# A two-layer attention kernel on one core: GpSimd issues its own store, maxima of a second unit go beside the last feed-forward, and one load of the output path comes sooner

## The chip, the cores and the metric

The kernel runs on one core of one Trainium2 chip. The metric is the device time of one execution in microseconds (us). Five engines matter: PE (TensorE, matmul), DVE (VectorE), ACT (ScalarE), POOL (GpSimd) and SP (SyncE, which here only issues DMA transfers). Each engine works through its own list of instructions strictly in order and waits on semaphores for the others.

## The reference

Two identical layers on x (4 batches of 512 tokens, width 320) with a context (4 x 1601 tokens, width 192). Each layer is self attention, cross attention and a gated feed-forward, each behind a layer norm and added to x; 20 heads of 16.

```python
h1 = _ln(x, n1_g, n1_b)
x = _attn(h1, h1, q1, k1, v1, o1_w, o1_b, heads) + x
h2 = _ln(x, n2_g, n2_b)
x = _attn(h2, context, q2, k2, v2, o2_w, o2_b, heads) + x
h3 = _ln(x, n3_g, n3_b)
proj = h3 @ ff_w1 + ff_b1
a, g = jnp.split(proj, 2, axis=-1)
ff = a * jax.nn.gelu(g, approximate=False) @ ff_w2 + ff_b2
return ff + x          # _attn: softmax(q k^T * 16**-0.5) v, then @ wo + bo
```

## The kernel before

**Units.** The attention is cut into units: one unit is four heads of one batch (five units a batch, so 20 self units and 20 cross units a layer, then four feed-forward units, `ff`). A self unit has 4 chunks of 128 keys, a cross unit 13. For each chunk PE makes the scores of four heads (tile `st`, line 1324), ACT takes their exponential (`pr`, L1334), and one chunk later PE multiplies by the values (`av`, L1350).

**Maxima.** The softmax subtracts each query's exact maximum, so before a unit can be scored, its scores are made once more only to be reduced: PE writes `sps` (L1076), DVE reduces it to `nmax` (self) or `pm` (cross) (L1087). A self unit has 16 such tiles, four to a round. `max_end` then turns the maxima into rows, and SP sends them to `nrows` (L1171, four small transfers a unit), which the next unit's scores need. `giver` decides whose maxima go beside the unit at work: `coming` are the units ahead, `ahead` those it may take; beside attention the rounds of maxima share the four row groups of PE with the scores, beside a feed-forward they stand alone.

**Sums.** A unit's `av` results are summed over its chunks in a tile `o`: the first chunk is copied by ACT (L1364), each later one is copied by ACT to `vo` (L1369) and added by POOL (L1370). There are two `o` tiles in turn, so the first copy of a unit must wait until the `o` of the unit before the last has been sent away. In the last unit before a feed-forward DVE does both.

**The output path** (`add_finish`). Everything in it goes through one chain named `divide`, first in, first out, with waits counted in rounds of the schedule (`since(i, n)`: n rounds after the i-th mark): `turn` sends `o` (128 x 512) to DRAM (`oway`, L1191, 256 KB); after the fifth unit of a batch `sums` loads the denominators (`den`, L1199), DVE inverts them, `read` loads the numerators and inverses back in three parts (`aT`, `rT`; L1224, L1225), POOL multiplies each part (L1232), and PE projects (`ops`, L1250) into x. The third part is loaded later than the first two, since its buffer is shared with the first. A `turn` that comes due while the third part is waiting stands behind it in the chain.

**Order.** The program is written out by hand by a planner at build time; it fixes the order on every engine. `nc.sync` transfers go out on SP in that order. POOL also makes the high and low halves of the projected q and k (L827, L828), the layer norm of later batches (`hturned`, L625) and bias additions (L618).

Of the kernel before, what the change touches and what calls it, by code (L numbers as in the profile page):

```python
# [25 lines left out]
G, HG = 5, 4  # L26
# [52 lines left out]
def kernel(ctx: ExitStack, tc: tile.TileContext, x, context, ws, out):  # L79
# [18 lines left out]
    nc = tc.nc  # L98
    dma = nc.sync.dma_start
# [313 lines left out]
    def bank(name):  # L413
        i = min(range(NB), key=lambda i: bank_free[i])
        assert bank_free[i] < HELD, name
        t = psum.tile([P, 512], F32, tag=f"bank{i}", name=name)
        bank_of[id(t)] = [i, t, bank_free[i], 0.0]
        bank_free[i] = HELD
        return t

    def written(us, *tiles):
        expect["pe"] = max([expect["pe"]] + [bank_of[id(t)][2] + 0.05 for t in tiles]) + us
        for t in tiles:
            bank_of[id(t)][3] = expect["pe"] + 0.17

    def busy(engine, us, *tiles):
        expect[engine] = max([expect[engine]] + [bank_of[id(t)][3] + 0.05 for t in tiles]) + us
        for t in tiles:
            bank_free[bank_of[id(t)][0]] = expect[engine] + 0.09
# [12 lines left out]
    def add(chain, cost, f, due, ready=yes, soon=yes):  # L442
        chains[chain].append((cost if isinstance(cost, tuple) else (cost,), due, ready, soon, f))
# [356 lines left out]
    def tiles_of(n):  # L800
        return [(f, min(SLOT, n - f)) for f in range(0, n, SLOT)]
# [377 lines left out]
    def add_finish(u):  # L1179

        when = [clock["round"]]

        def since(i, n):
            return lambda: len(when) > i and clock["round"] >= when[i] + n

        def turn():

            way = o_way[u.b % 2]  # L1190
            dma(out=way[:, u.g * HG : (u.g + 1) * HG].rearrange("s j n -> j s n"), in_=u.o)  # L1191
            if u.g == G - 1:
                held["written"] += 1
                errands.append((clock["round"] + 3, yes, sums))

        def sums():

            den = two.tile([P, N], F32, tag="rT", name="den")[:, : H * N // P]
            dma(out=den, in_=o_way[u.b % 2][DH].rearrange("h n -> (h n)").rearrange("(p c) -> p c", p=P))  # L1199
            when.append(clock["round"])  # L1200

            def invert():
                nc.vector.reciprocal(den, den)
                busy("dve", 0.75)
                when.append(clock["round"])

            def save():
                dma(out=r_way[u.b % 2].rearrange("h n -> (h n)").rearrange("(p c) -> p c", p=P), in_=den)
                errands.append((clock["round"] + 3, lambda: held["open"] < 1, read))

            add("divide", LIGHT, invert, r - 20, yes, since(1, 3))
            add("divide", 0.0, save, r - 20, yes, since(2, 1))

        def read():

            held["read"] += 1
            held["open"] += 1
            aT = one.tile([P, 3, N], F32, tag="aT", name="aT")
            way, part = o_way[u.b % 2], {}

            def load(k, at, n):
                heads = slice(at // DH, (at + n) // DH)
                part[k] = two.tile([P, N], F32, tag="rT", name="rT")
                dma(out=aT[:n, k, :], in_=way[:DH, heads])  # L1224
                dma(  # L1225
                    out=part[k][:n],
                    in_=r_way[u.b % 2][heads].rearrange("(o j) n -> o j n", o=1).to_broadcast([DH, n // DH, N]),
                )
                when.append(clock["round"])

            def divide(k, n):
                nc.gpsimd.tensor_tensor(aT[:n, k, :], aT[:n, k, :], part[k][:n], ALU.mult)  # L1232

            for k, at, n in DK[:2]:
                load(k, at, n)
            first, second, third = DK
            add("divide", 0.0, lambda: divide(0, first[2]), r - 20, yes, since(4, 3))
            add("divide", 0.0, lambda: divide(1, second[2]), r - 20)
            add("divide", 0.0, lambda: load(*third), r - 20, yes, since(4, 7))
            add("divide", 0.0, lambda: divide(2, third[2]), r - 20, yes, since(5, 3))  # L1240
            add("divide", 0.0, lambda: end(aT), r - 20)

        def project(aT, t, part):
            cols = slice(part * D // 2, (part + 1) * D // 2)
            ps = bank("ops")
            written(0.93, ps)
            busy("dve", 0.3, ps)
            for k, at, n in DK:
                for f, m in tiles_of(P):
                    nc.tensor.matmul(  # L1250
                        ps[f : f + m, : D // 2],
                        lhsT=aT[:n, k, f * NQ + t * SLOT : f * NQ + t * SLOT + m],
                        rhs=wo[:n, k, cols],
                        start=(k == 0),
                        stop=(k == 2),
                    )
            nc.vector.tensor_tensor(xs[u.b][:, t, cols], ps[:, : D // 2], xs[u.b][:, t, cols], ALU.add)

        def end(aT):
            now = clock["round"]  # L1260
            for t in range(NQ):
                for part in range(2):
                    add(
                        "project", (0.317,) * 3, lambda t=t, part=part: project(aT, t, part),
                        now + 2 + u.nch * t + u.nch // 2 * part, yes, lambda: clock["round"] >= now + 1,
                    )
            add("project", 0.0, done, now + 2 + u.nch * NQ)

        def done():
            held["open"] -= 1  # L1270
            after(u)

        r = when[0]
        add("divide", 0.0, turn, r - 20, lambda: u.g or held["written"] < held["read"] + 2, since(0, 2))


# [346 lines left out]
    def giver(u):  # L1623

        ahead, coming = [], []
        for v in units[u.i + 1 : u.i + AHEAD + 1]:
            if v.kind == "ff":
                break  # L1630
            coming.append(v)
            if v.i <= u.i + 2 and (v.i == u.i + 1 or u.kind != "ff") or v.early:
                ahead.append(v)
                if v.pairs is None:
                    v.pairs = max_pairs(v)
        owed = 0.0
        last = clock["round"]

        def give(h, alone=False):
            nonlocal owed, last  # L1640
            rounds = []
            went = clock["round"] - last if alone else 1
            last = clock["round"]
            total = 0
            most = 0.0
            urgent = None
            for v in coming:
                if v not in ahead:
                    total += v.steps
                    continue  # L1650
                total += left(v)


                rest = v.start - (7 if alone else 4) - clock["round"]
                if rest > 0:
                    most = max(most, (total - rest * (not alone)) / (2 * rest))
                if left(v) and (rest == 1 or alone and rest < 1):
                    urgent = urgent or v
                    owed = max(owed, 1.0 if alone and rest > -4 else (left(v) + 1) // 2)
            owed += most * went if total else 0.0  # L1660
            while owed >= 1.0 and any(left(v) for v in ahead) and not (alone and rounds and rest > -4):
                hand = [v for v in ahead if left(v) and all(v.pairs) and at_hand(v)]
                if not hand and ahead[0].start - 4 - clock["round"] > 1:
                    break
                v = hand[0] if hand else next(v for v in ahead if left(v))
                if u.kind == "self" and ahead[-1].early and urgent is None:

                    v = ahead[-1]
                    if v not in hand:
                        break  # L1670
                at_once(v)
                rounds.append([f for q in v.pairs if q for f in q.popleft()[1]])
                owed -= 1.0
            owed = min(owed, 2.0)
            for v in ahead:
                mine = v.pairs[h % 2]
                if mine and not alone and at_hand(v):
                    return mine.popleft(), rounds
            return (False, []), rounds

        return give
# [46 lines left out]
    for i, u in enumerate(units):  # L1728
# [10 lines left out]
        for k in (3, SOON, AHEAD):  # L1739
            v = units[i + k] if i + k < len(units) else None  # L1740
# [32 lines left out]
```

## Time and profile before

| | |
|---|---|
| three runs | 2933.25 us median (2932.35 to 2940.54) |
| profiled execution | 2933.88 us, of which its span is 2931.7 us |
| mean granted TensorE clock | 0.994 |
| busy in the span | PE 2863.0 us (98%), DVE 2069.9 (71%), ACT 1881.4 (64%), POOL 1299.4 (44%) |
| stages in the span | layer 0: self from 47 us, cross from 381, feed-forward from about 1214; layer 1: self from 1505, cross from 1837, feed-forward from about 2663 to the end |

The share of PE is the time in which some matmul was between its start and its modelled end, so a PE that waits in the middle of a matmul's issue still counts as busy; waits have to be looked for stage by stage. A wait is written as idle time with what ended it, for instance `[3.60 <-POOL aT L1232]`. SP's rows are the issues of transfers; a row of SP that takes several us for `x4` contains waits between its parts. A matmul on full fp32 stands in the trace as two instructions, so an `ops` row `x12` of the program's order is `x24` there.

### The profile page before, as it was taken

The numbers are of one execution on the slowest core, as the hardware profiler recorded it, in microseconds if no ns is written. First come the engines' busy times: TensorE is split into PE (matmuls) and PEld (weight loads), VectorE is DVE, ScalarE is ACT, GpSimd is POOL, SyncE is SP. The second block draws the span as 40 slices with busy tenths as digits, with TensorE's granted clock in tenths as the row PEclk, the third lists the DMA queues.
The fourth block names the chain that finished last, engine by engine and source line by source line (L and its number), as shares of the span: only waits on it lengthen the run. The fifth ranks groups of instructions, "written<-read, shape, count | busy, mean of one in ns | idle before, by whom it ended". The sixth has DMA issues, their size and how long they took to land.

```text
span 2931.7 us, 83446 instructions
## 1 busy us (share of the span) xinstructions
PE 2863.0 (98%) x35018; PEld 1540.3 (53%) x35018; DVE 2069.9 (71%) x4052; ACT 1881.4 (64%) x3733; POOL 1299.4 (44%) x1409
## 2 busy tenths in 40 slices
PE   8999999999999999999999999999999999999999
PEld 4445555555555555355554555555555555544554
DVE  6776888888888888323258678888888888872221
ACT  3767677887887888501138666778878778783000
POOL 3656345555545545211125663456455565551100
PEclk8999999999999999999999999999999999999999
DMA  3443223232232222200113342222221122222000
GB/s 106 113 120 99 68 73 101 59 85 62 49 93 61 54 54 62 84 17 11 42 38 88 99 104 69 58 62 53 62 65 47 50 72 51 53 56 76 22 20 14
DMA packets 163495, 188.59 MB, mean 64 GB/s; under 512 B 61988, under 2 KB 109104, under 8 KB 163120
## 3 DMA queue, kind: packets, MB, share of 16 engines
q1 hardware_dynamic: 162616, 181.69, 24.4%
q8 instruction: 275, 4.51, 0.6%
q10 hardware_dynamic: 472, 1.58, 0.2%
q14 instruction: 100, 0.82, 0.1%
q0 software_dynamic: 32, 0.00, 0.0%
HBM read 55.76 MB, written 29.36 MB: 29 GB/s over the span
## 4 chain that ended last, share of the span: by engine, by line
PE 87%; DVE 5%; POOL 2%; DMA 2%; ACT 2%; issue 1%; SPq 1%; ACTq 0%; POOLq 0%; DVEq 0%
PE av L1350 22%; PE st L1324 20%; PE fps L1435 10%; PE sps L1076 8%; PE yps L1542 6%; PE vps L1035 5%; PE kps L972 4%; PE ops L1250 4%; PE qkps L908 3%; PE fps L1495 3%; DVE nmax L1087 2%; PE qps L947 2%; DMA oway<-o 1%; PE sps L1101 1%; ACT pr L1334 1%
## 5 line engine op out<-in xcount | busy, mean ns | idle before, releaser
L1334 ACT ACTIVATE pr<-st 128x512 f32<-128x512 f32 (+1 forms) x2720 | 1404.5, 604 | 394.3 <-PE st L1324 359.3
L1087 DVE TENSOR_REDUCE pm<-sps 128x1 f32<-128x512 f32 (+1 forms) x1920 | 1147.8, 660 | 138.7 <-PE sps L1076 132.4
L1370 POOL TENSOR_TENSOR o<-o,vo 128x512 f32<-128x512 f32 x576 | 739.8, 1284 | 950.8 <-ACT vo L1369 942.0
L1076 PE MATMUL sps<-kT,q 32*128 32x512 f32 (+1 forms) x4800 | 869.0, 421 | 12.2 <-DMA q<-halves 4.4
L1324 PE MATMUL st<-q,kT 32*128 32x512 f32 (+1 forms) x5120 | 790.7, 420 | 2.8 <-ACT o L1364 2.4
L1350 PE MATMUL av<-pr,vals 128*32 128x512 f32 (+1 forms) x5440 | 734.5, 606 | 35.0 <-ACT pr L1334 13.4
L1324 PEld LDWEIGHTS st<-q,kT 32*128 32x128 f32 (+1 forms) x5120 | 448.5, 180 | 297.4 <-ACT pr L1334 117.5
L1324 PE MATMUL st<-nrows,ones 32*128 32x512 f32 (+1 forms) x2720 | 560.6, 399 | 4.8 <-DMA nrows<-turned 4.7
L1076 PEld LDWEIGHTS sps<-kT,q 32*128 32x128 f32 x4800 | 429.8, 184 | 73.7 <-DVE nmax L1087 14.6
L1087 DVE TENSOR_REDUCE nmax<-sps 128x1 f32<-128x512 f32 x640 | 396.7, 682 | 92.7 <-PE sps L1076 89.2
L1369 ACT COPY vo<-av 128x512 f32<-128x512 f32 x576 | 353.0, 613 | 17.4 <-PE av L1350 10.3
L1506 ACT ACTIVATE gl<-fps,b 128x512 f32<-128x512 f32 x80 | 54.7, 687 | 408.9 <-PE fps L1495 299.1
L1435 PE MATMUL fps<-hT,w 128*128 128x512 f32 x640 | 283.1, 597 | 0.0
L1350 PEld LDWEIGHTS av<-pr,vals 128*32 128x32 f32 (+1 forms) x5440 | 110.9, 108 | 309.9 <-DVE pm L1087 175.8
L1324 PEld LDWEIGHTS st<-nrows,ones 32*128 32x128 f32 (+1 forms) x2720 | 264.6, 180 | 14.8 <-DMA nrows<-turned 6.0
L1507 DVE SCALAR_TENSOR_TENSOR hid<-fps,b,gl 128x512 f32<-128x512 f32 x80 | 59.7, 748 | 242.6 <-ACT gl L1506 240.5
L1435 PEld LDWEIGHTS fps<-hT,w 128*128 128x128 f32 x640 | 119.2, 190 | 155.1 <-issue 152.2
L1542 PE MATMUL yps<-w,hid 128*128 128x320 f32 x640 | 175.5, 434 | 0.0
L1542 PEld LDWEIGHTS yps<-w,hid 128*128 128x128 f32 x640 | 120.6, 190 | 56.1 <-ACT gl L1506 5.3
L1250 PEld LDWEIGHTS ops<-wo,aT 112*32 112x32 f32 (+1 forms) x3072 | 99.3, 111 | 63.1 <-issue 29.5
L1250 PE MATMUL ops<-wo,aT 112*32 112x160 f32 (+1 forms) x3072 | 126.1, 302 | 5.5 <-POOL aT L1232 5.0
L527 POOL TENSOR_SCALAR root<-root 128x4 f32<-128x4 f32 x22 | 5.2, 234 | 266.8 <-DVE root L521 266.7
(91 smaller groups left out, 2544.1 us busy)
## 6 DMA issues: line engine op xcount, KB each, us to landing
kT<-stages SPq DMA_DIRECT2D x80, 400.5 KB
oway<-o SPq DMA_DIRECT2D x80, 256.0 KB
q<-halves SPq DMA_DIRECT2D x80, 256.0 KB
q<-halves SPq DMA_DIRECT2D x27, 512.0 KB
kT<-halves SPq DMA_DIRECT2D x40, 256.0 KB
aT<-oway SPq DMA_DIRECT2D x32, 224.0 KB
rT<-rway SPq DMA_DIRECT2D x32, 224.0 KB
hT<-hturned SPq DMA_DIRECT2D x96, 64.0 KB
```

Of the source, the lines that this page charges most:

```text
L972: nc.tensor.matmul(ps[(i * GT + f) * SLOT : (i * GT + f + 1) * SLOT, :w], lhsT=wk2[:, k, u.g * GD + f * SLOT : u.g * GD + (f + 1) * SLOT], ...
L1035: nc.tensor.matmul(ps[f : f + m, :w], lhsT=u.kvT[:n, k, at + f : at + f + m], rhs=wv[:n, k, h0 * DH : h1 * DH], start=(k == 0), stop=(k == ...
L1076: nc.tensor.matmul(own[0][:, :w], lhsT=u.queries(slice(j * SLOT, (j + 1) * SLOT), e, t), rhs=u.kT[j * SLOT : (j + 1) * SLOT, u.k0 + at : u ...
L1087: nc.vector.tensor_reduce(to, own[0][:, :w], AX.X, ALU.max)
L1250: nc.tensor.matmul(ps[f : f + m, : D // 2], lhsT=aT[:n, k, f * NQ + t * SLOT : f * NQ + t * SLOT + m], rhs=wo[:n, k, cols], start=(k == 0) ...
L1324: nc.tensor.matmul(own[0][:r, :], lhsT=ones[rows, :r] if e == 2 else u.keys(rows, c), rhs=u.rows[rows, :] if e == 2 else u.queries(rows, e ...
L1334: nc.scalar.activation(p[:r], own[0][:r], AF.Exp)
L1350: nc.tensor.matmul(ps[j * SLOT : (j + 1) * SLOT, :], lhsT=columns_of[:r, head : head + SLOT], rhs=pr.pop((c, j))[:r, :], start=True, stop= ...
L1369: nc.scalar.copy(vo, ps)
L1370: nc.gpsimd.tensor_tensor(u.o, u.o, vo, ALU.add)
L1435: nc.tensor.matmul(ps, lhsT=w1[:, k, i * FF + c * P : i * FF + (c + 1) * P], rhs=natural(u.hT[:, k]), start=start, stop=stop,)
L1542: nc.tensor.matmul(ps[:, :D], lhsT=hid[c][:, t * P : (t + 1) * P], rhs=w2[:, c, :], start=(c == 0), stop=(c == NHC - 1),)
```

## The change

Three edits. In `turn`, POOL issues the transfer of `o` itself instead of SP (80 transfers, all of them). In the output path the third load comes 5 instead of 7 rounds after its mark in layer 1; in layer 0 it stays at 7. In `giver`, a feed-forward unit may take the maxima of the next two units instead of the next one; only the last feed-forward of layer 0 has attention units ahead.

```diff
         def turn():

             way = o_way[u.b % 2]
-            dma(out=way[:, u.g * HG : (u.g + 1) * HG].rearrange("s j n -> j s n"), in_=u.o)
+            nc.gpsimd.dma_start(out=way[:, u.g * HG : (u.g + 1) * HG].rearrange("s j n -> j s n"), in_=u.o)
...
-            add("divide", 0.0, lambda: load(*third), r - 20, yes, since(4, 7))
+            add("divide", 0.0, lambda: load(*third), r - 20, yes, since(4, 5 if u.l else 7))
...
-            if v.i <= u.i + 2 and (v.i == u.i + 1 or u.kind != "ff") or v.early:
+            if v.i <= u.i + 2 or v.early:
                 ahead.append(v)
```

**Place A: PE, end of layer 0's last feed-forward and first unit of layer 1.** `yps` is the second feed-forward product, `q_102`, `q_103` and `q_104` are the queries of the first, second and third self unit of layer 1; `-` is the kernel before, `+` the changed one.

```order
 L1542 MATMUL yps<-w_22016,hid 128x320 x4
+L1076 MATMUL sps<-kT_101,q_103 128x512 x8
 L1542 MATMUL yps<-w_22016,hid_22439 128x320 x3
 L1542 MATMUL yps<-w_22016,hid_22440 128x320 x3
 L1542 MATMUL yps<-w_22016,hid 128x320 x4
+L1076 MATMUL sps<-kT_101,q_103 128x512 x8
 L1324 MATMUL st<-q_102,kT_101 128x512 x2
```

```order
 L1350 MATMUL av<-pr,vals 32x512 x4
-L1076 MATMUL sps<-kT_101,q_103 128x512 x8
-L1076 MATMUL sps<-kT_101,q_104 128x512 x16
+L1076 MATMUL sps<-kT_101,q_104 128x512 x8
 L1324 MATMUL st<-q_102,kT_101 128x512 x2
```

Two rounds of four maxima of the second unit now stand before and behind the last `yps` of the feed-forward. One lone round in the first chunk of unit 0 (eight matmuls of a row `x10`) is gone, and the three lone rounds behind its second chunk have become one; the last four maxima of the third unit are done in the first chunk of unit 1. Unit 0 has 5 rounds of maxima instead of 8, not counting the two that moved.

**Place B: the transfer of unit 12's sums in layer 0.** Before, on SP: `o_4279` is the sum of unit 12, `o_4550` of unit 13, the `halves` are the split k and q of later units, the `aT`/`rT` rows are the third load of batch 1.

```order
L1224 DMA aT_4375<-oway1_131 96x1x512
L1225 DMA rT_4625<-rway1_133 96x1x512
L876 DMA kT0_101<-halves_4298 128x1x512
L876 DMA q1_103<-halves_4298 128x1x1024
L1191 DMA oway0_130<-o_4279 4x32x512
L876 DMA q3_136<-halves_4565 128x1x512 x2
L1191 DMA oway0_130<-o_4550 4x32x512
```

The same transfers in the changed kernel, on POOL:

```order
L1370 TENSOR_TENSOR o_4550<-o_4550,vo_4622 128x512
L1370 TENSOR_TENSOR o_4550<-o_4550,vo_4673 128x512
L1370 TENSOR_TENSOR o_4550<-o_4550,vo_4723 128x512
L1232 TENSOR_TENSOR aT_4375<-aT_4375,rT_4625 96x512
L1191 DMA oway0_130<-o_4279 4x32x512
L1191 DMA oway0_130<-o_4550 4x32x512
L827 CAST halves_4791<-halves_4791 128x512
```

Unit 12's transfer has moved behind all of unit 13's additions and the third multiplication on POOL. At the same place of layer 1 the third multiplication and unit 12's transfer stand between the second and the third of those additions.

**Place C: POOL, units 8 and 9 of layer 1**, before and then changed. `o_26178` and `o_26165` are the sum of unit 8, `hturned` is the layer norm of batch 3, `oway1_131<-o_25872` the transfer of unit 7.

```order
L1370 TENSOR_TENSOR o_26178<-o_26178,vo_26254 128x512
L625 TENSOR_SCALAR hturned_26115<-x3_110,mv_25804,root2_25977 128x4x32
L625 TENSOR_SCALAR hturned_26115<-x3_110,mv_25804,root2_25977 128x3x32 x2
L827 CAST halves_26199<-halves_26199 128x512
L828 TENSOR_TENSOR halves_26199<-halves_26199 128x512
L1370 TENSOR_TENSOR o_26178<-o_26178,vo_26321 128x512
L1232 TENSOR_TENSOR aT_25912<-aT_25912,rT_26180 96x512
```

```order
L1370 TENSOR_TENSOR o_26165<-o_26165,vo_26238 128x512
L1232 TENSOR_TENSOR aT_25896<-aT_25896,rT_26099 96x512
L1191 DMA oway1_131<-o_25872 4x32x512
L625 TENSOR_SCALAR hturned_26102<-x3_110,mv_25788,root2_25961 128x4x32
L625 TENSOR_SCALAR hturned_26102<-x3_110,mv_25788,root2_25961 128x3x32 x2
L827 CAST halves_26183<-halves_26183 128x512
L828 TENSOR_TENSOR halves_26183<-halves_26183 128x512
L1370 TENSOR_TENSOR o_26165<-o_26165,vo_26307 128x512
```

The third multiplication comes one piece of layer norm, one split into halves and one addition sooner, and the transfer follows it. On PE the first `ops` of that batch comes one chunk sooner too.

## Prediction

> **What bounds the kernel now.** I read the totals of the page first, then the waits, then the groups by line.
>
> ```profile
> span 2931.7 us, 83446 instructions
> PE 2863.0 (98%) x35018; PEld 1540.3 (53%) x35018; DVE 2069.9 (71%) x4052; ACT 1881.4 (64%) x3733; POOL 1299.4 (44%) x1409
> ACT o L1364 <- DMA oway<-o: 7.6, 2, 3.9
> PE ops L1250 <- POOL aT L1232: 5.0, 2, 3.6
> ACT vo L1369 <- POOL o L1370: 5.8, 6, 2.7
> SPq L1191 <- POOL o L1370: 311.0, 65, 10.5
> SPq L1171 <- DMA oway<-o: 6.0, 4, 2.3
> ```
>
> A row of waits gives the sum, the count and the longest. PE is the bound: its visible idle time is 2931.7 − 2863.0 = 68.7 us, and no PE work is removed. So a gain can only come from waits of PE that these edits end, and each is a few us. SP stands 311.0 us behind POOL's additions, 65 times, because it issues the `oway` transfers in order; that costs PE only where something behind them on SP is urgent, the `nrows` transfers above all. So the places to look at are `nrows` late behind `oway`, `aT` late, ACT's first copy waiting for `oway`, ACT waiting for POOL's additions, and, seen in no wait of PE, the unit behind the feed-forward.
>
> **The second edit: maxima beside the last feed-forward.** The trace by time, PE and DVE around unit 0 of layer 1, then two windows (columns as in the heading; the clock is PEclk):
>
> ```profile
> 1493.33 0.74 PE L1076 MATMUL sps<-kT,q 32*128 32x512 f32 x8
> 1494.00 11.03 PE L1542 MATMUL yps<-w,hid 128*128 128x320 f32 x40
> 1529.19 0.50 PE L1324 MATMUL st<-q,kT 32*128 32x512 f32 x2
> 1499.69 0.49 DVE L1549 TENSOR_TENSOR x<-yps,x 128x320 f32<-128x320 f32 x1 [3.10 <-PE yps L1542]
> 1505.75 14.44 DVE L1087 TENSOR_REDUCE nmax<-sps 128x1 f32<-128x512 f32 x24 [0.18 <-PE sps L1076]
> core 0: us, PE busy (x) PEld busy (x) DVE busy (x) ACT busy (x) POOL busy (x), PEclk, DMA share, GB/s
> 1515.80:1526.00 10.20, 10.20 (x57) 4.78 (x56) 9.10 (x18) 4.21 (x9) 2.03 (x2) 0.50 0.02 2
> 1529.20:1543.40 14.20, 13.91 (x213) 7.53 (x210) 10.62 (x20) 11.15 (x23) 9.19 (x10) 1.00 0.21 50
> ```
>
> Unit 0 runs from the end of `yps` (1494.00 + 11.03 = 1505.03) to the first `st` of unit 1 (1529.19): 24.2 us, against 14.2 us for unit 1. DVE bounds it: 24 reduces back to back take 14.44 us (0.602 each), eight more follow, and PE, starved, gets a clock of 0.50 with 57 matmuls in 10.2 us. After the change eight of these 32 reduces lie elsewhere: four beside the last `yps`, where DVE stands idle 3.10 us, four in unit 1, where DVE is busy 10.62 of 14.20 us. That takes 8 × 0.602 = 4.8 us off; one more round of `sps` alone on PE costs 0.74; a shorter half-clock stretch I put at 1.1 (about a fifth of the 5.1 us which that stretch costs). T1 = 4.8 − 0.7 + 1.1 = **+5.2** (plus is a gain). Bounds: 0, if the wait only moves to unit 1; 9.4, if nine tenths of those 5.1 us end (4.6 + 4.8) and the lone round is hidden.
>
> **The first edit: what SP gains.** POOL sends `oway` behind its own last addition, so nothing waits there any more, and SP is free for `nrows`. The trace around two late `nrows`:
>
> ```profile
> 162.14 1.12 SPq L1191 DMA_DIRECT2D oway<-o  x1
> 166.97 4.89 SPq L1171 DMA_DIRECT2D nrows<-turned  x4
> 175.44 0.50 PE L1324 MATMUL st<-nrows,ones 32*128 32x512 f32 x2 [2.32 <-DMA nrows<-turned]
> 193.64 2.12 PE L1250 MATMUL ops<-wo,aT 96*32 96x160 f32 x56 [1.36 <-POOL aT L1232]
> 1801.59 0.50 PE L1324 MATMUL st<-nrows,ones 32*128 32x512 f32 x2 [1.14 <-DMA nrows<-turned]
> ```
>
> The four `nrows` issues of a unit take 4.89 us here, since the fourth shares a semaphore with the `oway` transfer issued at 162.14 and waits for its landing (so I read the 6.0 us, 4 times, of `SPq L1171` above). With `oway` on POOL's own queue that ends. PE waited 2.32 and 1.14 us for those rows. Of the 2.32, 1.0 comes back at 193.64, where PE waits for POOL's `aT`, which doesn't come sooner by the whole: 1.3. With 1.1 at 1801.59, T2 = **+2.4** (0 if another wait stands behind each, 3.5 if both go whole).
>
> **The third edit: third load two rounds sooner in layer 1.**
>
> ```profile
> 1642.86 1.29 POOL L1370 TENSOR_TENSOR o<-o,vo 128x512 f32<-128x512 f32 x1
> 1644.11 2.24 POOL L625 TENSOR_SCALAR hturned<-x,mv,root 128x128 f32<-128x128 f32 x3
> 1649.38 1.26 POOL L1232 TENSOR_TENSOR aT<-aT,rT 96x512 f32<-96x512 f32 x1
> 1650.69 2.12 PE L1250 MATMUL ops<-wo,aT 96*32 96x160 f32 x56 [3.60 <-POOL aT L1232]
> ```
>
> The third product at 1649.38 stood behind an addition, the layer norm, a split and another addition. In the new order it stands right behind the addition of 1642.86, so it can end at 1642.86 + 1.29 + 1.26 = 1645.4. PE came to it at 1650.69 − 3.60 = 1647.1; its `ops` now stand one chunk sooner (14.2 / 4 = 3.5 us by unit 1 above), so it comes at about 1643.6 and waits some 1.6 us for the product: T3 = 3.6 − 1.6 = **+2.0** (0, if the loads land later than the buffer, to 3.6).
>
> **The first edit: what a transfer loses behind POOL's work.** Units 12 of both layers are those where ACT waits for a transfer.
>
> ```profile
> 275.36 0.66 SPq L1191 DMA_DIRECT2D oway<-o  x1
> 280.29 1.30 POOL L1232 TENSOR_TENSOR aT<-aT,rT 96x512 f32<-96x512 f32 x1
> 284.96 0.58 ACT L1364 COPY o<-av 128x512 f32<-128x512 f32 x1 [3.93 <-DMA oway<-o]
> 285.60 0.73 PE L1324 MATMUL st<-q,kT 32*128 32x512 f32 x3 [1.36 <-ACT o L1364]
> 604.10 0.57 SPq L1191 DMA_DIRECT2D oway<-o  x1
> 609.89 0.36 SPq L1199 DMA_DIRECT2D den<-oway  x1
> 1732.44 0.88 SPq L1191 DMA_DIRECT2D oway<-o  x1
> 1733.41 1.28 POOL L1370 TENSOR_TENSOR o<-o,vo 128x512 f32<-128x512 f32 x1 [1.24 <-ACT vo L1369]
> 1741.77 0.58 ACT L1364 COPY o<-av 128x512 f32<-128x512 f32 x1 [3.67 <-DMA oway<-o]
> ```
>
> In layer 0 the transfer goes out at 275.36, lands about 284.9, and ACT's copy waits 3.93 us for it, PE 1.36 behind ACT. Now it stands behind the product of 280.29, that is 281.6. A transfer with nothing beside it took 609.89 − 604.10 = 5.79 us. So it lands about 287.4, with POOL's issue some 0.4 longer than SP's (below) 287.8, which is 2.9 us later, and PE, whose slack is used up already, goes with it: T4 = **−2.9**. Ends: −6, if it lands as slowly as before (9.5 us); +1.4, PE's whole wait, if it lands in the 1.8 us of the one transfer that POOL issues now (below).
>
> In layer 1 it went out at 1732.44 and landed about 1741.7. Now it stands behind the addition of 1733.41 (end 1734.7) and a product of 1.27: 1736.0, plus 5.79, is 1741.8. T5 = **0**. Ends: −2, if it takes 2 us more, as beside other transfers in layer 0; +3.7, the whole wait, if it lands fast.
>
> **POOL's 80 issues.** Groups by line (min/median/max in ns): the single POOL transfer with its landing, SP's 80, and POOL's additions; then the sizes, POOL's queue, and one tight stretch (columns as above):
>
> ```profile
> L1171 POOL DMA_DIRECT2D nrows<-turned x1: 763/763/763, 39.6 to 39.6; - x1
> DMA to landing us min/median/max: 1.8/1.8/1.8
> L1191 SPq DMA_DIRECT2D oway<-o x80: 548/582/2341, 72.1 to 2662.2; - x80
> L1370 POOL TENSOR_TENSOR o<-o,vo 128x512 f32<-128x512 f32 x576 | 739.8, 1284 | 950.8 <-ACT vo L1369 942.0
> oway<-o SPq DMA_DIRECT2D x80, 256.0 KB
> q0 software_dynamic: 32, 0.00, 0.0%
> 255.00:275.00 20.00, 19.82 (x232) 9.95 (x224) 14.59 (x27) 17.29 (x34) 18.48 (x21) 1.00 0.41 114
> ```
>
> No row shows POOL sending 128 rows of 2 KB. The one it sends, 32 packets, took 763 ns; I take 1.0 us, nearest to that and above it for four times the rows. Ends: 0.58, SP's; 3.05, if each row costs as much as there (4 × 0.763). POOL idles 950.8 us before its additions, and most issues stand right behind a unit's last addition with 2 to 8 us of idle time behind them: they cost nothing. The cover is thin where layer norm and splits fill POOL (for a moment about 114 and 1573; from 255 to 275, where it is busy 18.48 of 20 us, and at the same place of layer 1). There an addition comes later by what is left of the issue, and ACT's next `vo` waits for the addition before (the 5.8 us, 6 times, of `ACT vo` above), so ACT comes later with it. When I lay 1.0 us behind the last addition, product or norm piece ahead of each issue and push POOL's rows on until idle time takes it up, ACT's copies come later by 0.7, 0.6 and 1.5 us in the tight places of a layer, some 3 us, 6 in both. How much of that PE passes on, no row tells; between none and all I take half: T6 = **−3.0**. Ends: 0, and −20, by 3.05 us an issue with T4 and T5 later by 2.0 each.
>
> **Sum.** 5.2 + 2.4 + 2.0 − 2.9 + 0 − 3.0 = +3.7. The profiled execution took 2933.88 us (its span and 2.2 around it), so 2930.2; the median of the runs is 0.6 below it: **2929.6 us**. 0.3% (8.8 us) is about what a measurement can tell from no change, and this is inside it.
>
> **Rivals.** First, transfers from POOL land fast everywhere, as the only one of them did (1.8 us): T4 is +1.4 and T5 +3.7, the sum 5.2 + 2.4 + 2.0 + 1.4 + 3.7 − 3.0 = 11.7, so about 2921.5, faster by 0.4%. For it speaks that row; against it, that it was 32 packets, and these are 256 KB.
>
> The Trainium skill ("DMA: Bandwidth & Descriptors", section "Anatomy of one DMA — SWDGE (gpsimd) path") fits 2.0 us plus bytes over 436,000 per us to a transfer that GpSimd issues; as an estimate from that page, 256 KB take 2.6 us, and the sum would be near this rival's. The 5.79 us above are of SP's issue, so no row here decides it. The same page (section "Why a DMA increments its semaphore by 16 and not by 1") speaks against a gain: the slowest dimensions set how many engines share a transfer, by one rule for both issuers, and here these are 4 and 128, so four of 16 whoever issues; by it the forecast's 5.79 us stays.
>
> Second, on the other side: the issue costs by the rows, 3.05 us. ACT's delays in the tight places then add up to some 33 us by the same working, half is 16.5, and T4 and T5 lose 2.0 each: 5.2 + 2.4 + 2.0 − 2.9 − 4.0 − 16.5 = −13.8, about 2947. From about 1.6 us an issue the change is a loss, from about 2.7 it is slower by 0.3%. For it: 763 ns for only 32 packets. Against: that row is one sample, and a part of it is likely the same for any size, as SP's two issues at 604 and 609 us, 0.57 for `oway` and 0.36 for the smaller `den`, differ by little.
>
> Third, the second edit does nothing: the four reduces that go to unit 1 and PE's low clock only move by one unit, T1 is 0, 2935. For it: unit 1 has its own maxima; against, DVE has 3.6 us free in it.
>
> **Chances.** Forecast 0.50, fast transfers 0.20, costly issues 0.12, no gain of the second edit 0.18. Faster takes the first rival and a tenth of the forecast (T1 near 9): 0.26; slower most of the second and a little of the third: 0.12; the rest, 0.62, is within. The range goes from 2918 (first rival, with T1 a little higher) to 2940 (T6 at 2 us an issue), and leaves out the worst of the second rival and a T1 at its upper end with fast transfers, together under 2 in 10.
>
> **What would show it.** T1: the run of reduces behind 1505 has 20 or fewer, and unit 0 lasts about 19 us. T2: no wait of PE for `nrows` near 173 and 1800. T3: the wait of `ops` near 1648 is about 1.5. T4: ACT's wait for `oway` near 282 grows to about 6.7. T5: the one near 1741 stays. T6: issues of L1191 on POOL take about 1 us, and ACT's wait for POOL's `o` grows by a few us from 5.8. It would be wrong if the landing from POOL is far from 5.8 us or the issue far from 1.0 us.

## The result, and the profile after

The changed kernel takes 2945.55 us (median; 2943.7 to 2947.22) against 2932.07 for the kernel before beside it. The ratio is 1.0039, 95% interval 1.0028 to 1.0049: slower by 11 us (8 to 14), or 13.5 by the two medians, where 3.7 us faster was forecast. The profiled execution has a span of 2944.5 us against 2931.7, 12.8 longer.

The totals of the page of the changed kernel, then the rows of its waits that answer to those of before (sum, count, longest), then its line 1191 (issue time in ns, and time from issue to landing):

```profile
span 2944.5 us, 83482 instructions
PE 2867.1 (97%) x35018; PEld 1539.3 (52%) x35018; DVE 2068.2 (70%) x4046; ACT 1884.4 (64%) x3739; POOL 1355.4 (46%) x1489
```

```profile
ACT o L1364 <- DMA oway<-o: 11.7, 4, 7.4
PE st L1324 <- DMA nrows<-turned: 7.9, 8, 2.0
PE st L1324 <- ACT o L1364: 5.0, 1, 5.0
ACT vo L1369 <- POOL o L1370: 4.1, 6, 2.6
PE ops L1250 <- POOL aT L1232: 3.3, 3, 1.6
POOL oway L1191 <- POOL o L1370: 15.6, 48, 1.0
```

```profile
L1191 POOL DMA_DIRECT2D oway<-o x80: 688/713/765, 71.9 to 2675.0; - x80
...
DMA to landing us min/median/max: 5.8/7.0/11.5
```

Two rows of the waits of before belong beside these:

```profile
PE st L1324 <- DMA nrows<-turned: 4.7, 5, 2.3
PE st L1324 <- ACT o L1364: 2.4, 2, 1.4
```

PE does the same 35018 matmuls, so the loss is waits, some of them inside what counts as busy. ACT's wait for `oway` grew from 7.6 to 11.7 us with one wait of 7.4, and PE's for `nrows` from 4.7 to 7.9, while the waits for POOL's product (5.0 to 3.3) and for POOL's additions (5.8 to 4.1) shrank. POOL's issue is short, 0.71 us; the landing is 7.0 us, longer than the 5.79 of SP's isolated transfer. The time by stage, before and then after (windows with the columns as in the prediction, the length first; self and cross units of layer 0, then of layer 1):

```profile
47.50:381.30 333.80, 318.73 (x4624) 172.30 (x4620) 253.50 (x504) 235.05 (x469) 169.07 (x197) 0.99 0.38 97
381.30:1181.30 800.00, 785.56 (x11297) 432.17 (x11290) 686.27 (x1327) 645.29 (x1295) 429.59 (x408) 1.00 0.27 68
1505.50:1837.40 331.90, 318.01 (x4484) 171.02 (x4480) 256.23 (x501) 230.46 (x458) 169.97 (x199) 0.98 0.34 87
1837.40:2629.30 791.90, 781.21 (x11296) 432.03 (x11292) 676.59 (x1289) 643.37 (x1289) 429.07 (x407) 1.00 0.23 58
```

```profile
47.30:387.80 340.50, 320.04 (x4624) 172.55 (x4620) 253.75 (x504) 235.08 (x469) 182.40 (x216) 0.98 0.38 95
387.80:1191.40 803.60, 786.87 (x11296) 432.83 (x11292) 686.37 (x1327) 645.07 (x1293) 442.23 (x426) 1.00 0.28 68
1517.90:1843.30 325.40, 313.61 (x4489) 170.06 (x4492) 252.44 (x495) 231.12 (x460) 183.62 (x218) 0.98 0.36 89
1843.30:2641.90 798.60, 783.92 (x11276) 430.01 (x11268) 674.86 (x1284) 645.46 (x1293) 441.95 (x426) 1.00 0.24 58
```

Layer 0 loses 6.7 us in its self units and 3.6 in its cross units; layer 1 gains 6.5 in the self units and loses 6.7 in the cross units. Unit by unit (from the first `st<-nrows` of one unit to that of the next) the larger differences are:

```
unit (what waits there)                    before  after   difference
layer 0 self  3 (nrows)                     13.90  16.19   +2.3
layer 0 self  7 (the nrows behind oway)     17.67  16.35   -1.3
layer 0 self 11 (nrows)                     17.77  19.11   +1.3
layer 0 self 14 (oway of unit 12)           23.55  26.99   +3.4
layer 0 cross 6 (ctxT)                      46.08  49.22   +3.1
layer 0 cross 11 (ctxT)                     45.07  46.23   +1.2
layer 1 self  0 (maxima)                    24.23  19.72   -4.5
layer 1 self  3 (nrows)                     13.35  15.63   +2.3
layer 1 self  8 and 9 (third product)       37.17  36.17   -1.0
layer 1 self 14 (oway of unit 12)           23.33  21.19   -2.1
```

A trace is one execution. In the traces of the second edit, the third and both together, which have transfers on SP and the same layer 0 as before, units 3 and 11 of layer 0 keep their length within 0.02 us, but units 7, 9 and 14 and cross unit 7 differ from this table's "before" by up to 3.0 us. A difference of that size in one of the latter is not shown by one pair of traces.

Three kinds of places lose. First, unit 12's transfer in layer 0. The changed kernel's trace by time:

```profile
283.86 1.30 POOL L1232 TENSOR_TENSOR aT<-aT,rT 96x512 f32<-96x512 f32 x1
285.10 1.44 POOL L1191 DMA_DIRECT2D oway<-o  x2
...
292.26 0.58 ACT L1364 COPY o<-av 128x512 f32<-128x512 f32 x1 [7.43 <-DMA oway<-o]
...
292.90 0.79 PE L1324 MATMUL st<-q,kT 32*128 32x512 f32 x2 [5.04 <-ACT o L1364]
```

POOL issues it at 285.10, right behind the product, it lands 7.1 us later at 292.2, and ACT and PE stand. Second, `nrows` beside a transfer that now lies later and lasts longer:

```profile
105.59 2.61 SPq L1171 DMA_DIRECT2D nrows<-turned  x4
...
106.80 0.76 POOL L1191 DMA_DIRECT2D oway<-o  x1
...
114.73 0.49 PE L1324 MATMUL st<-nrows,ones 32*128 32x512 f32 x2 [1.96 <-DMA nrows<-turned]
```

The last of these four small transfers, issued at 107.6, lands at 114.7, 7.1 us later; before, the one issued at 108.0 landed 3.7 us later, at 111.6. Both times it lands just behind the `oway` that it meets, 0.2 us behind POOL's (114.5) and 0.7 behind SP's (110.9). Third, the context's `ctxT` beside the transfer of cross unit 5; rows of DVE and PE of before, then the changed kernel:

```profile
657.56 0.64 DVE L757 STREAM_TRANSPOSE stages<-stages 128x192 f32<-128x192 f32 x2 [1.55 <-DMA ctxT<-stages]
658.77 1.03 PE L1250 MATMUL ops<-wo,aT 112*32 112x160 f32 x24 [0.50 <-DVE pm L1087]
```

```profile
653.69 0.71 POOL L1191 DMA_DIRECT2D oway<-o  x1
658.09 2.77 SPq L765 DMA_DIRECT2D ctxT<-stages  x1
665.97 0.64 DVE L757 STREAM_TRANSPOSE stages<-stages 128x192 f32<-128x192 f32 x2 [3.22 <-DMA ctxT<-stages]
667.17 1.03 PE L1250 MATMUL ops<-wo,aT 112*32 112x160 f32 x24 [2.17 <-DVE pm L1087]
```

SP had sent that `oway` at 643.03, and it had landed at 649.3, before `kT` and `ctxT` went out. On POOL it stands behind a split of `stages` and the third product, 10.7 us later where the kernel as a whole lags by 6.7, so `stages`, `kT` and `ctxT` meet it; `ctxT` takes 7.8 us to land instead of 6.1, DVE waits for it, DVE's maxima come late and PE waits for DVE, 2.17 us instead of 0.50. That meeting `oway` is what makes it late is not shown, though: in the run below whose transfers land fast, this `oway` had landed at 646.7, before `ctxT` went out at 648.8, and `ctxT` still took 7.5 us and cross unit 6 was still 2.6 us longer than before.

### The profile page after: what moved, and what is told of

The parts are those of the page before. It is cut to its first block, busy times and chain, and to the rows that moved or that the text cites. A ratio compares the mean times of both kernels' runs of the same rounds, so it can differ in the third digit from the quotient of the medians.

```text
span 2944.5 us, 83482 instructions
## 1 busy us (share of the span) xinstructions
PE 2867.1 (97%) x35018; PEld 1539.3 (52%) x35018; DVE 2068.2 (70%) x4046; ACT 1884.4 (64%) x3739; POOL 1355.4 (46%) x1489
## 3 DMA queue, kind: packets, MB, share of 16 engines
q0 software_dynamic: 21792, 21.10, 3.2%
## 4 chain that ended last, share of the span: by engine, by line
PE 84%; DVE 5%; POOL 3%; DMA 3%; ACT 2%; issue 2%; SPq 1%; POOLq 0%; ACTq 0%; DVEq 0%
PE av L1350 21%; PE st L1324 19%; PE fps L1435 10%; PE sps L1076 8%; PE yps L1542 6%; PE vps L1035 5%; PE kps L972 3%; PE ops L1250 3%; PE qkps L908 3%; PE fps L1495 2%; DVE nmax L1087 2%; DVE pm L1087 2%; PE qps L947 2%; ACT pr L1334 1%; PE sps L1101 1%
## 5 line engine op out<-in xcount | busy, mean ns | idle before, releaser
L1076 PE MATMUL sps<-kT,q 32*128 32x450 f32 (+1 forms) x4800 | 867.9, 422 | 13.1 <-DVE vals L1014 4.5
L1324 PE MATMUL st<-q,kT 32*128 32x512 f32 (+1 forms) x5120 | 792.2, 421 | 5.8 <-ACT o L1364 5.0
L1324 PEld LDWEIGHTS st<-q,kT 32*128 32x128 f32 (+1 forms) x5120 | 447.9, 180 | 299.9 <-ACT pr L1334 114.3
L1324 PE MATMUL st<-nrows,ones 32*128 32x512 f32 (+1 forms) x2720 | 561.7, 400 | 9.9 <-DMA nrows<-turned 7.9
L1324 PEld LDWEIGHTS st<-nrows,ones 32*128 32x128 f32 (+1 forms) x2720 | 264.3, 180 | 22.4 <-DMA nrows<-turned 7.9
L908 PE MATMUL qkps<-hT,wqk 96*32 96x256 f32 (+1 forms) x1920 | 118.8, 390 | 0.8 <-DVE nmax L1087 0.8
```

The source lines that it names most:

```text
L908: nc.tensor.matmul(ps[f : f + m, :w], lhsT=wqk[:n, k, f // GD, column : column + m], rhs=first.hT[:n, k, at : at + w], start=(k == 0), sto ...
L1076: nc.tensor.matmul(own[0][:, :w], lhsT=u.queries(slice(j * SLOT, (j + 1) * SLOT), e, t), rhs=u.kT[j * SLOT : (j + 1) * SLOT, u.k0 + at : u ...
L1324: nc.tensor.matmul(own[0][:r, :], lhsT=ones[rows, :r] if e == 2 else u.keys(rows, c), rhs=u.rows[rows, :] if e == 2 else u.queries(rows, e ...
```

## The experiments

All are compared with the kernel before on the same chip. The theory that the trace of the changed kernel gave is A: the transfers of POOL land late and make others land late, and PE waits at a few places. Its rival is B: POOL's time and its order cost, whatever the transfer does.

**One edit at a time.** The first edit alone is the `turn` line of the diff on the kernel before.

> The kernel before with the first edit alone: GpSimd issues the 80 transfers of o, loads and maxima as before. Both theories put the loss here. Theory A (landing): a transfer that POOL issues lands 7.0 us after its issue instead of 5.8, and the small nrows transfers that go out beside it land late (7.1 instead of 3.7 us at 108 us); PE waits for them. Theory B (place): POOL's issue, 0.72 us each, and the places in POOL's order delay additions, products and unit 12's transfer. Both: 14 to 20 us slower than before (2947 to 2953), that is the +13 of all three edits and the some 5 us which the other two save. A third reading, that the second and third edits cause the loss, would give 2930 to 2935 here.

Measured: 2953.19 us, ratio 1.0074 (1.0061 to 1.0086). Its waits:

```profile
ACT o L1364 <- DMA oway<-o: 19.0, 5, 7.7
PE st L1324 <- ACT o L1364: 10.1, 2, 5.1
```

The first edit is the whole loss, and more than all three together. The 10.1 us of PE behind ACT are two places, unit 12 in both layers.

The changed kernel with the transfers back on SP:

```diff
-            nc.gpsimd.dma_start(out=way[:, u.g * HG : (u.g + 1) * HG].rearrange("s j n -> j s n"), in_=u.o)
+            dma(out=way[:, u.g * HG : (u.g + 1) * HG].rearrange("s j n -> j s n"), in_=u.o)
```

> The changed kernel with the transfers of o back on SP: second and third edits alone. If the first edit causes the loss: 2926 to 2930, some 4 us faster than before (unit 0 of layer 1 shorter by 4.5, one lone round of sps 1.3 dearer, the wait for the third product about 1 to 2 shorter). If the other edits cause it: 2940 and above.

Measured: 2927.99 us, ratio 0.9985 (0.9976 to 0.9994). The other two edits together are worth 2 to 7 us. Against this kernel the first edit costs 1.0039 − 0.9985 = 0.54%, some 16 us.

The second edit alone (`giver`) and the third alone (`since(4, 5 if u.l else 7)`), each on the kernel before:

> The kernel before with the second edit alone (a feed-forward may take the maxima of two units). By the changed kernel's trace unit 0 of layer 1 goes from 24.2 to 19.7 us (4.5 less) and the lone round beside the last yps costs 1.3: 3.2 faster, about 2929.5. If the reduces only move to unit 1: 2932 to 2934.

> The kernel before with the third edit alone (third load at 5 rounds in layer 1). Two edits together took 4.7 off; with 3.2 for the second, this one is worth 1 to 2: 2931 to 2932. If the wait for the third product went altogether, 2929. A rival: its gain is larger with POOL issuing, since it also takes a transfer forward; then it is about 1.5 here and 7 there.

Measured: 2932.47 us, 0.9999 (0.9987 to 1.0010), and 2933.25 us, 0.9997 (0.9986 to 1.0008). Neither is told from no change; for each, a gain of up to about 4 us is not excluded. Layer 1's self units with the second edit, then self and cross units with the third:

```profile
1507.40:1840.60 333.20, 319.14 (x4461) 171.77 (x4465) 252.56 (x494) 231.18 (x460) 169.92 (x199) 0.97 0.34 87
```

```profile
1505.40:1831.30 325.90, 315.75 (x4505) 171.70 (x4501) 256.19 (x503) 230.26 (x457) 170.56 (x199) 0.98 0.35 88
1831.30:2628.10 796.80, 783.22 (x11272) 430.32 (x11268) 674.74 (x1284) 645.42 (x1293) 429.25 (x407) 1.00 0.23 57
```

With the second edit unit 0 takes 16.95 us, 7.3 less than before, and still the self units take 333.2 us, 1.3 more: unit 9 takes 26.67 instead of 23.88, unit 14 25.15 instead of 23.33, and unit 18 4.1 more. Not all of that is the edit's: unit 9 is longer by 2.9 us in the trace of the first edit alone too, and by 2.4 in that of the new layout alone (below). With the third the self units gain 6.0 us, and the cross units, whose order it also moves, take 796.8 instead of 791.9, so 4.9 are given back. The cross units come out alike in the other trace with SP issuing that has the third edit (797.0 us with the second and third), so this is the order's and not chance; why they are slower in it I did not find out.

**The first and third edit together**, without the second:

> First and third edits, without the second. The third edit alone measured nothing (0.9997); with POOL issuing it also brings unit 12's transfer of layer 1 two additions forward, where the first edit alone lost 4.7. If the edits interact there: 2946 to 2949, 4 to 7 us below the first edit alone. If they add up: 2952 to 2954.

Measured: 2948.59 us, 1.0062 (1.0049 to 1.0075). The median is 4.6 below the first edit alone, as by the interaction, but the intervals overlap, so it isn't shown by the times. In the trace it is seen: PE waits for ACT at one place instead of two (`PE st L1324 <- ACT o L1364` is 5.1 us, once).

**POOL's time alone.** Behind SP's issue, on the kernel before, with `idle_t` an unused 128 x 4 tile:

```diff
             dma(out=way[:, u.g * HG : (u.g + 1) * HG].rearrange("s j n -> j s n"), in_=u.o)
+            for _ in range(4):
+                nc.gpsimd.tensor_tensor(idle_t, idle_t, idle_t, ALU.mult)
```

> The kernel before, transfers on SP, and four small multiplications of an unused 128 x 4 tile on POOL (about 0.2 us each) behind each issue's place: POOL's time alone, some 0.8 us 80 times. Prediction's term T6 scaled to 0.8 us: 2 to 3 us slower, 2935 to 2936. If POOL's time is what costs: 2940 and above. If it is hidden: 2932 to 2934.

```profile
L1195 POOL TENSOR_TENSOR idle_t<-idle_t 128x4 f32<-128x4 f32 x320 | 64.1, 200 | 19.1
```

Measured: 2937.71 us, 1.0015 (1.0005 to 1.0026), for 0.80 us of work 80 times (64.1 us, with 19.1 idle ahead of it). This lies between what was expected of T6 and what was expected if POOL's time is the cause. So 0.8 us of POOL costs 1.5 to 7.6 us, and POOL's 0.71 us with its wait of 0.3 for its own addition (15.6 us in 48) can be no more than a part of the 18 to 25 of the first edit.

**The place alone.** SP issues, but not before POOL has come to the place:

```diff
+            nc.gpsimd.tensor_copy(out=u.o[:, :1], in_=u.o[:, :1])
             dma(out=way[:, u.g * HG : (u.g + 1) * HG].rearrange("s j n -> j s n"), in_=u.o)
```

> The kernel before, transfers on SP, but POOL copies one column of o onto itself at the place where the changed kernel issues the transfer, so that SP's transfer can't go out sooner than POOL's would. This has the place in POOL's order, SP's landing (5.8 us) and 0.2 us of POOL instead of 0.72; it also makes SP wait for POOL where POOL is late, which the first edit doesn't. Theory A (landing): the place is the smaller part, 2935 to 2940. Theory B (place): close to the first edit alone, 2947 to 2953. Since SP's waiting is added, a large loss would not settle it, a small one would.

```profile
ACT o L1365 <- DMA oway<-o: 13.4, 3, 6.6
```

Measured: 2959.94 us, 1.0091 (1.0075 to 1.0107), against the expectation of A. As said ahead, a large loss does not settle it, since SP, with `nrows` behind, waits here too; it does say that a transfer at POOL's places, with SP's landing, isn't free. One place can be read without SP's waiting: for the transfers of unit 12, which land here in 5.8 us, ACT waits 6.65 and 6.64 us, against 3.93 and 3.67 before and 7.67 and 7.47 with the first edit alone. There the place makes most of the longer wait, and the slower landing from POOL the last 1 us of it.

**The landing alone.** `oway` is laid out head by head, so that the same 256 KB are 128 rows in one dimension; POOL issues at the same places:

```diff
-    o_way = [dram.tile([SLOT, H, N], F32, name=f"oway{i}") for i in range(2)]
+    o_way = [dram.tile([H, SLOT, N], F32, name=f"oway{i}") for i in range(2)]
...
-            nc.gpsimd.dma_start(out=way[:, u.g * HG : (u.g + 1) * HG].rearrange("s j n -> j s n"), in_=u.o)
+            nc.gpsimd.dma_start(out=way[u.g * HG : (u.g + 1) * HG].rearrange("j s n -> (j s) n"), in_=u.o)
...
-            den = two.tile([P, N], F32, tag="rT", name="den")[:, : H * N // P]
-            dma(out=den, in_=o_way[u.b % 2][DH].rearrange("h n -> (h n)").rearrange("(p c) -> p c", p=P))
+            den = two.tile([P, N], F32, tag="rT", name="den")[: H * NQ, :P]
+            dma(out=den, in_=o_way[u.b % 2][:, DH].rearrange("h (q c) -> h q c", c=P))
...
-                dma(out=r_way[u.b % 2].rearrange("h n -> (h n)").rearrange("(p c) -> p c", p=P), in_=den)
+                dma(out=r_way[u.b % 2].rearrange("h (q c) -> (h q) c", c=P), in_=den)
...
-                dma(out=aT[:n, k, :], in_=way[:DH, heads])
+                dma(out=aT[:n, k, :], in_=way[heads, :DH].rearrange("h s n -> s h n"))
```

> The changed kernel with oway laid out head by head (20 x 32 x 512 instead of 32 x 20 x 512), so that a transfer of o is 128 rows in one dimension instead of 4 x 32; den is loaded as 80 partitions of 128. POOL still issues at the same places. Theory A: the transfer spreads over more engines, lands in about 3 us, nrows behind it in under 3: most of the 13 us loss goes, 2926 to 2935. Theory B: POOL's issues and places are the same, so 2941 to 2947.

Line 1191 of that kernel, and the rows of POOL's queue, of the changed kernel and then of this one:

```profile
L1191 POOL DMA_DIRECT2D oway<-o x80: 542/584/633, 71.8 to 2660.7; - x80
...
DMA to landing us min/median/max: 2.2/2.6/6.3
```

```profile
q0 software_dynamic: 21792, 21.10, 3.2%
```

```profile
q0 software_dynamic: 6432, 20.98, 1.8%
```

Measured: 2929.55 us, 0.9991 (0.9981 to 1.0000). The landing falls from 7.0 to 2.6 us and the kernel is no longer slower than before, with POOL's places unchanged and its issue only 0.13 us shorter. But the layout gains with SP issuing too, so the first edit's price in this layout is the distance to the same kernel with SP issuing (0.9976, under "A better version"): 0.15%, some 4 us, where it is 0.54%, some 16 us, in the old layout. So about three quarters of the price need the transfer that takes 7 us: the places cost that much only together with it. The remaining quarter is about what 0.8 us of POOL's time cost above. The layout also changes the loads of `den` and `aT`, and the `aT` loads stand ahead of the third product; by the semaphore records of the two traces they land in about the same time (medians 3.7 and 3.5 us for `aT`, 2.1 and 2.4 for `den`).

What the shape changes can be read from the updates of the transfer's semaphore. For the first transfer of a kernel, at 72 us: from POOL in 4 x 32 rows, twelve of sixteen updates come 1.83 to 2.06 us after the issue and the last four at 5.15 to 6.50; in 128 rows, fifteen come at 2.14 to 2.34 and the last at 3.79. From SP in 4 x 32 rows there is one update at 1.00 and four at 5.45 to 5.75; in 128 rows, sixteen from 1.81 to 1.98. So in 4 x 32 rows the data comes with four late updates, in 128 rows with none or one. The 128 rows also lie next to each other in DRAM, which the 4 x 32 do not; the runs do not separate the two.

**Which transfers.** The first edit alone, with a few transfers left on SP (`back`):

```diff
+            back = not u.cross and (u.b, u.g) == (2, 2)
-            dma(out=way[:, u.g * HG : (u.g + 1) * HG].rearrange("s j n -> j s n"), in_=u.o)
+            (nc.sync if back else nc.gpsimd).dma_start(out=way[:, u.g * HG : (u.g + 1) * HG].rearrange("s j n -> j s n"), in_=u.o)
```

> First edit alone, but the transfer of self unit 12 of both layers back on SP (2 of 80). With the first edit alone ACT's first copy waits 7.7 us for that transfer, PE 5.1 and 5.0 behind it, against 1.4 and 1.1 before. If these two places carry their share: 8 to 10 us come back of the 20.5, 2943 to 2945. If the loss is spread over all transfers (issue time, landing): 2 of 80 give nothing, 2951 to 2954.

Measured: 2941.16 us, 1.0032 (1.0019 to 1.0044). Two transfers of 80 carry 1.0074 − 1.0032 = 0.42%, some 12 us, more than the 8 to 10 expected; unit 14 is 6.1 us shorter in layer 0 and 7.2 in layer 1 than with the first edit alone. With ten of them back:

```diff
+            back = (u.b, u.g) in (((1, 0), (2, 0)) if u.cross else ((0, 2), (2, 0), (2, 2)))
```

> First edit alone, but ten transfers back on SP: self units 2, 10 and 12 and cross units 5 and 10 of both layers. These are the ones beside which, in the trace, nrows (112, 250, 1584 and 1722 us) or the context's ctxT (665 and 876 us) landed late or ACT waited. If the loss is of single collisions: nearly all comes back, 2931 to 2936, with the gains of the freed SP (the nrows waits at 173 and 1800, about 3) kept. If it is spread: one eighth comes back, 2950.

Its waits (its lines are one further down):

```profile
ACT o L1365 <- DMA oway<-o: 3.9, 3, 2.7
PE ops L1251 <- POOL aT L1233: 3.8, 2, 3.0
PE st L1325 <- DMA nrows<-turned: 2.7, 4, 1.5
```

Measured: 2933.58 us, 1.0005 (0.9994 to 1.0016). The loss is in five transfers of each layer, picked from the trace by who stood behind them: with these back it can no longer be told from none, and the other 70, less what the freed SP gains, cost 5 us at most. Since landing, place and queue all went back together, this says which transfers cost, not by which of the three.

**A better version.** The layout head by head with SP issuing, on the kernel before and with the second and third edits:

> The kernel before with oway laid out head by head, nothing else: SP's transfer lands in about 2 us instead of 5.8. The waits of ACT for oway (7.6) go, of which PE had 2.4, and nrows behind a transfer comes sooner: 2 to 5 us faster, 2927 to 2930. If only the second and third edits made the wide kernel faster: 2932.

> Second and third edits, transfers of o on SP, oway laid out head by head as in the run with POOL's issue. Theory A: with SP's transfers landing in about 2.5 us instead of 5.8 to 9.5, the waits of ACT for oway (7.6 us) and of PE for nrows (4.7) shrink as well: 2920 to 2927, 2 to 6 us below the same edits in the old layout. Theory B: landing matters little, equal to that kernel within 2 us.

Measured: 2925.24 us, 0.9975 (0.9966 to 0.9984), and 2924.75 us, 0.9976 (0.9967 to 0.9985). Both are about 7 us faster than the kernel before, the first by more than the 2 to 5 expected; on top of the layout the second and third edits add nothing that can be told. In the first of them (line 1191, then the wait for `nrows`):

```profile
L1191 SPq DMA_DIRECT2D oway<-o x80: 320/329/1805, 71.4 to 2655.6; - x80
```

```profile
PE st L1324 <- DMA nrows<-turned: 0.7, 1, 0.7
```

ACT's wait for `oway` is gone from its list of waits (for unit 12 of layer 0 the copy still waits 1.05 us, which the list puts down to PE but which ends 0.08 us behind the landing), and PE's for `nrows` is 0.7 instead of 4.7 us.

## Why the prediction was wrong, point by point

- **The step that failed: the first edit's price.** The sum has it at 2.4 − 2.9 + 0 − 3.0 = −3.5 (T2, T4, T5, T6); measured with the same other edits it is 0.54%, some 16 us. The other two edits, 7.2 us in the sum, gave 2 to 7 together, so the first edit holds most of the error, some 12 us of 15. The prediction costed a moved transfer for those who wait for it (T4, T5) and for SP's queue (T2), and had no term for what a transfer that goes out later, and is in flight longer, does to the small urgent ones that it meets. In the table, `nrows` in units 3 and 11 of layer 0 and unit 3 of layer 1 are +2.3, +1.3 and +2.3, together 5.9 us, and these three units are within 0.02 us of before in the traces with the transfers on SP, with ten of them back and with the fast landing. And T4 was put too low: unit 14 is +3.4 in the table, +6.2 against the trace with the transfers on SP. Together these are 9 to 12 of the 16 us. The rest is not traced place by place; POOL's time, some 4 us by the run on it (T6's 3.0), would about fill it.
- **T1, +5.2: right in kind, too high in the sum.** Unit 0 of layer 1 is 4.5 us shorter (DVE's run of 24 reduces became one of twelve and smaller ones), and 7.3 with the edit alone. But the stretch ahead of it, from the last cross unit of layer 0 through the feed-forward, is 2.3 us longer in the traces with the edit and 0.1 to 0.6 in those without, so the moved rounds cost some 2 us there, where 0.7 was put for one. And alone the edit measured between 3.8 us faster and 2.9 slower, so 5.2 did not reach the end. A gain in one unit was carried to the end as it stood; in that trace units 9, 14 and 18 are longer, but unit 9 is so without the edit as well, so where it goes is open.
- **T2, +2.4: the waits right, the gain not shown.** The four issues are no longer held up, and what is left of PE's wait is 1.01 us of 2.32; unit 7 is 1.3 shorter and unit 9, where PE waits for `aT`, 0.7 longer. But with SP issuing and the other two edits, the same layer 0, these units are 2.2 shorter and 2.2 longer, so these traces don't show it to be the first edit's doing. The wait at 1801 is gone; the unit there is 0.4 shorter, and 1.3 with the first edit alone. The rows near 173:

```profile
168.03 2.67 SPq L1171 DMA_DIRECT2D nrows<-turned  x4
...
176.17 0.49 PE L1324 MATMUL st<-nrows,ones 32*128 32x512 f32 x2 [1.01 <-DMA nrows<-turned]
```

- **T3, +2.0: about right at its place.** PE waits 1.40 instead of 3.60 us, units 8 and 9 together are 1.0 shorter (by the prediction's own figures the wait is 1645.4 − 1643.6 = 1.8 and T3 1.8). Alone, the edit gains 6.0 us in the self units, more than at its place, and loses 4.9 in the cross units, whose order the prediction did not look at.

```profile
1654.69 0.48 PE L1250 MATMUL ops<-wo,aT 96*32 96x160 f32 x8 [1.40 <-POOL aT L1232]
```

- **T4, −2.9: right mechanism, too small.** ACT waits 7.43 us instead of 3.93 (6.7 was said), and unit 14 is 3.4 longer, 6.2 longer than with the transfers on SP. The landing measured 7.1 where 5.8 was taken. (With a landing of 9.5 and POOL's 0.4 the lower end is −6.6, not −6.)
- **T5, 0: too low.** ACT's wait at this place is 1.56 instead of 3.67 us, and the unit 2.1 shorter. With the first edit alone it is 7.47 and the unit 4.9 longer: here it is the third edit, which brings the transfer forward, that helps. With SP issuing and both other edits ACT doesn't wait here at all.

```profile
1751.04 0.58 ACT L1364 COPY o<-av 128x512 f32<-128x512 f32 x1 [1.56 <-DMA oway<-o]
```

- **T6, −3.0: right in size, wrong in the wait.** The issue takes 0.71 us, with 0.3 ahead of it in 48 of 80, about the 1.0 that was taken; 0.8 us of other work on POOL measured 1.5 to 7.6, and POOL's issue in place of SP's some 4 in the new layout. But ACT's wait for POOL's additions fell to 4.1 where it was to grow.
- **The rivals.** Fast landing (1.8 us) is refuted: 7.0. Costly issues, at about 2947, came near the measured time by luck: the issue took 0.71 us, not 3.05. That the second edit does nothing fits the run with it alone, though its local gain came.

The Trainium skill ("DMA: Bandwidth & Descriptors", "Anatomy of one DMA — SWDGE (gpsimd) path") gives, as an estimate by its fit, 2.6 us for 256 KB; the trace agrees for the 128 rows in one dimension (2.6) and not for 4 x 32 rows (7.0). The rule of the same page that weighs against it ("Why a DMA increments its semaphore by 16 and not by 1": the slowest dimensions set the number of engines) names what differs between these two kernels, and the trace agrees with it: the landings are 7.0 and 2.6 us, and with 4 x 32 rows four updates of the semaphore come late, the four engines of that rule.

## What to carry to other kernels

Before a transfer is moved to another queue, list what it will be in flight with at the new time, not only who waits for it: with the first edit alone two of the 80 transfers carried some 12 us, more than POOL's time for all 80. Look at the shape of a slow transfer before its issuer: one dimension of 128 rows instead of 4 x 32 was worth 7 us on the kernel before and 14 on the changed one, more than any of the three edits. A gain in one unit of an order written out by a planner has to be followed to the end of the stage, since it can be given back there; and a gain that is read from one pair of traces has to be looked for in others, since units of one and the same program differed by up to 3 us here.

## What the runs showed of the hardware

- The same 256 KB in 4 x 32 rows land in 7.0 us (median) from POOL and in 5.8 from SP; in 128 rows of one dimension in 2.6 from POOL and, by the semaphore records of the trace, in 2.0 from SP.
- POOL's queue carries 272 packets for each transfer of 4 x 32 rows (21792 less the 32 of before, over 80) and 80 for each of 128 rows; its issue takes 0.71 and 0.58 us.
- With 4 x 32 rows four of the semaphore's updates come at 5.2 to 6.5 us from POOL (the other twelve by 2.1) and at 5.5 to 5.8 from SP; with 128 rows from SP all sixteen come by 2.0.
- A 4 KB `nrows` that lands in 1.7 us by itself took 7.1 beside a transfer of POOL's queue, and 3.7 beside one of SP's own: it landed 0.2 and 0.7 us behind the large one. Separate queues did not keep them apart.
